# Mamba stage: which states turn by plain products, and where the input projection's last step stands

## The chip, the cores and the metric

The kernel runs on one core of a Trainium2 chip. The metric is the device time of one execution in microseconds (us). A core has a matrix engine (TensorE, PE in the profile, with its weight loads shown as PEld), a vector engine (VectorE, DVE), an activation engine (ScalarE, ACT), a general engine (GpSimd, POOL) and queues for DMA transfers. The engines run side by side, each through its own list of instructions, and wait for one another by semaphores. TensorE writes to PSUM, a small memory of banks that VectorE and ScalarE read; everything else stands in SBUF. The profile also says which share of its full clock TensorE was granted.

## The reference

The program is a vision model of four layers on a tensor of 2 images x 256 channels x 32 x 32: a stage of two Mamba blocks, a local attention by dilated 7x7 convolution, linear attention with a mixture of experts, and softmax attention with a mixture of experts. Only the Mamba stage is touched here. Its core is, for each of the two blocks:

```python
xs, res = split(u @ in_w + in_b)              # 1024 tokens per image, 512 inner channels each
xs = silu(causal_conv4(xs) + conv_b)
dt, Bm, Cm = split(xs @ xproj_w)              # 16, 16 and 16 columns
delta = softplus(dt @ dt_w + dt_b)
dA = exp(delta[..., None] * A)                # 16 states for each channel
dBu = delta[..., None] * Bm[:, :, None, :] * xs[..., None]
hst = dA_t * hst + dBu_t                      # token after token
y_t = einsum('bdn,bn->bd', hst, C_t)
out = ((y + xs * Dp) * silu(res)) @ out_w + out_b
```

The block's output is normed and added to its input; the second block sees the channels in reverse order.

## The kernel before

**Units and slots.** `layer0` (L710) goes over eight units, u0 to u7: two blocks of four chunks of 512 tokens each. For each unit `Mamba.scan` (L488) goes over 16 states and, within a state, four groups of 128 channels: 64 slots, numbered 0 to 63 as 4n + dc. In each slot ScalarE writes the decay exp(delta A) of one state and one group into one of three PSUM banks (m_da, L558), and VectorE runs the recurrence over 512 tokens with one scan instruction (L562), in place over m_h. GpSimd has filled m_h with delta B x before, 1024 columns at a time (L174), into six buffers, which is three states.

**Turning a state.** The scan leaves a state as channels x tokens, but its weighting with C is by token. So `rest(n)` (L507) turns it: four groups (one for each 128 tokens) of four 128x128 pieces, on TensorE, into a ring of three PSUM banks (m_ht). It runs during the slots of the next state: state 7 in slots 32 to 35, 10 in 44 to 47, 11 in 48 to 51, 13 in 56 to 59, and 14 in 60 to 63; state 15 falls into slots 0 to 3 of the next unit. Line 515 chooses between two ways of turning a piece. For a state in `PLAIN` (L264) it is an ordinary matmul with the identity as the moving operand (L516), which in 32-bit floats is two instructions; otherwise it is a transpose (L518), which is one. VectorE then multiplies the group by C's column and adds it to m_ya (L532); for states 0, 3, 6 and 9 ScalarE does this step (L530).

**What runs between.** After each slot's scan the code takes one step of `before` (the turning of the last state) and one of `between`, a list made by `paced` (L687): each entry is a generator with the number of steps to take, the first slot and the end, and the steps are spread evenly between these. The entries are:

- `front` of the next chunk: the convolution with four diagonal taps (m_conv, L373), silu, the projection to dt, B and C (m_xd_ps, L395), the delta matmuls (m_dt, L431), and ScalarE's functions for softplus (L436 and L440 for each of four groups, then L445, L447, L452, L454);
- `enter` of the chunk after that: the input projection, four steps of two matmuls with 512 columns (m_in, L343), each with a copy by ScalarE (m_pre, L347). In u0 to u5 the four steps stand at slots 37 to 45 (`ENTER`, L782);
- `back` of the chunk before: the gate (m_g, L590), the sum (m_y, L619 and L624; read by L628), the output projection (m_out, L635 and L639), its batch-norm statistics on VectorE (L183), and the norm's transposes (mm_t, L204);
- weights of the convolution of the next layer, turned on TensorE (w1t, L871; taps_ps, L877).

The last unit has no next chunk. In its place it carries the early part of the next layer's convolution (early_acc, L933), 112 steps in slots 3 to 63.

**What sets the order.** The code's order above is the wish; a tile scheduler then puts each engine's instructions into a queue, so that an edit can also move neighbours. Each engine then works its queue in order.

Of the kernel before, what the change touches and what calls it, by code (L numbers as in the profile page):

```python
# [258 lines left out]
class Mamba:  # L259
# [1 line left out]


    ADDED = 3, 6, 9
    PLAIN = 10, 13, 14  # L264
    LATER = 3
    ENTER = 4
    HEAD = 12
# [220 lines left out]
    def scan(self, j, before, between, start=False, last=False):  # L488

        net, nc, m, scanp = self.net, self.net.nc, self.m, self.scanp
        xs, bd, ct, delta, du = self.chunks[j]
        state, first = self.state, self.first(j)
        ya = self.two.tile([P, TPC, DI], F32, tag="ya", name=f"{m}_ya_{j}")
        yb = self.one.tile([P, TPC, DI], F32, tag="yb", name=f"{m}_yb_{j}")
        self.chunks[j] = xs, ya, yb
        G = 2  # L500
        half = [P, G, TC]

        def keep(n, hs):
            for g, h in enumerate(hs):
                nc.scalar.copy(state[:, n, g * G : (g + 1) * G], h[:, :, TC - 1])

        def rest(n, hs):  # L507


            for i in range(TPC):  # L510
                ps = self.ps_ht.tile([P, DI], F32, tag="ht", name=f"{m}_ht_{j}_{n}_{i}")
                for dc in range(NDC):
                    a = ps[:, dc * P : (dc + 1) * P]
                    h = hs[dc // G][:, dc % G, i * P : (i + 1) * P]
                    if n in self.PLAIN:
                        nc.tensor.matmul(a, lhsT=h, rhs=net.ident, start=True, stop=True)  # L516
                    else:
                        nc.tensor.transpose(a, h, net.ident)  # L518
                yield
                c = ct[:, i, n : n + 1]  # L520
                to = ya if n == 0 else None
                if n in self.ADDED:
                    if i == 0:
                        aside = self.tail(f"{m}_s_{j}_{n}")[:, : TPC * DI]
                        self.due[n + self.LATER] = (
                            yb, aside.rearrange("p (i d) -> p i d", d=DI), n != self.ADDED[0]
                        )
                    to = self.due[n + self.LATER][1]
                if to is not None:
                    nc.scalar.activation(to[:, i, :], ps, AF.Copy, scale=c)  # L530
                else:
                    nc.vector.scalar_tensor_tensor(  # L532
                        ya[:, i, :], ps, c, ya[:, i, :], ALU.mult, ALU.add
                    )
                if i == 0 and first:
                    keep(n, hs)

        for n in range(NS):
            b = scanp.tile([P, TC], F32, tag="b", name=f"{m}_b_{j}_{n}", bufs=4)
            nc.sync.dma_start(b, bd[n].partition_broadcast(P))  # L540
            hs = []
            for g in range(NDC // G):
                h = scanp.tile(half, F32, tag="h", name=f"{m}_h_{j}_{n}_{g}", bufs=6)
                factors = du[:, g * G : (g + 1) * G, :], b.unsqueeze(1).to_broadcast(half)
                if start and n == 0:
                    nc.vector.tensor_mul(h, *factors)
                else:
                    net.lined(nc.gpsimd.tensor_mul, h, *factors)
                hs.append(h)
            if n in self.due:  # L550
                to, a, add = self.due.pop(n)
                op = ALU.add if add else ALU.bypass
                net.lined(nc.gpsimd.dma_start, to, a, accum_op=op)
            for dc in range(NDC):
                da = self.ps_da.tile([P, TC], F32, tag="da", name=f"{m}_da_{j}_{n}_{dc}")
                i = dc * NS + n
                with net.tc.issue_after(net.loaded.ins):
                    net.decayed = nc.scalar.activation(  # L558
                        da, delta[:, dc, :], AF.Exp, scale=self.aneg[:, i : i + 1]
                    )  # L560
                h = hs[dc // G][:, dc % G, :]
                nc.vector.tensor_tensor_scan(  # L562
                    h, da, h, 0.0 if first else state[:, n, dc : dc + 1], ALU.mult, ALU.add
                )


                next(before, None)
                if n or dc:
                    next(between, None)
            before = chain(before, rest(n, hs))  # L570
        for _ in between:
            pass
        self.due = {} if last else {self.LATER: (ya, yb, True)}
        return before
# [135 lines left out]
def layer0(net, x, x_dram, m1, m2, load_image, taps, conv_dram, lg):  # L710
# [5 lines left out]
    with (  # L716
# [34 lines left out]
        for u, (m, j) in enumerate(units):  # L751
# [4 lines left out]
            steps = [(b, NDC, 4, 20) for b in done]  # L756
# [9 lines left out]
            enters = []  # L766
# [12 lines left out]
            for n, first, end in Mamba.STEPS:  # L779
                steps += [(f, n, first, end) for f in fronts]  # L780
            steps += [(b, 8, 48, 56) for b in done]
            steps += [(e, Mamba.ENTER, 37, 45) for e in enters]  # L782
            steps += [(b, 2, 1, 4) for b in late] + [(b, 2, 9, 15) for b in late]
            steps += [(b, 1, 57, 58) for b in done]
            if u + 1 == len(units):
# [993 lines left out]
def conv_attn_hybrid(ctx: ExitStack, tc: tile.TileContext, a: dict, out: bass.AP):  # L1779
# [6 lines left out]
    with tc.tile_pool(name="conv_w", bufs=2) as convw:  # L1786
        def load_x(b):
            for cc in range(NCC):
                nc.sync.dma_start(x[:, cc, b, :], a["x"][b, cc])

        load_x(0)
        taps = Taps(net, convw, main, x, a["l1_w1"], a["l1_w2"])
        layer0(
            net, x, a["x"],
            [a[f"m1_{k}"] for k in ("in_w", "out_w", "xproj_w", "dt_w")],
            [a[f"m2_{k}"] for k in ("in_w", "out_w", "xproj_w", "dt_w")],
            lambda: load_x(1), taps, conv_dram, lg,
        )
# [117 lines left out]
```

## Time and profile before

| | before |
|---|---|
| median of 3 runs (lowest to highest) | 2128.23 us (2127.43 to 2129.8) |
| the profiled execution's own time | 2127.49 us |
| its span, first to last instruction | 2125.8 us |
| busy: TensorE, VectorE, ScalarE, GpSimd | 1882.2, 1373.1, 900.9, 1042.0 us |
| mean granted TensorE clock | 0.933 |
| Mamba stage: first scan, last scan | 51.4 us, 1018 us |
| lengths of u0 to u7, first scan to next first scan | 108.8, 120.1, 119.9, 122.1, 114.5, 118.2, 114.7, 148.3 us |

In the table, a unit's length runs from its first scan to that of the next unit, and for u7 to the end of its last scan. A line of groups in the profile names the code line, the engine, the operation, its output and inputs, and the shape with its count; then the busy time and the mean length of one; then the engine's idle time just ahead of these instructions and what ended it. A line of waits names the waiting engine and line, whom it waited for, the sum, the number and the longest. A line of a timeline gives the start, the length and the instruction, with the number of like ones in a row; in brackets stands the idle time ahead of it.

### The profile page before, as it was taken

The numbers are of one execution on the slowest core, as the hardware profiler recorded it, in microseconds if no ns is written. First come the engines' busy times: TensorE is split into PE (matmuls) and PEld (weight loads), VectorE is DVE, ScalarE is ACT, GpSimd is POOL, SyncE is SP. The second block draws the span as 40 slices with busy tenths as digits, with TensorE's granted clock in tenths as the row PEclk, the third lists the DMA queues.
The fourth block names the chain that finished last, engine by engine and source line by source line (L and its number), as shares of the span: only waits on it lengthen the run. The fifth ranks groups of instructions, "written<-read, shape, count | busy, mean of one in ns | idle before, by whom it ended". The sixth has DMA issues, their size and how long they took to land.

```text
span 2125.8 us, 27536 instructions
## 1 busy us (share of the span) xinstructions
PE 1882.2 (89%) x9812; PEld 1352.4 (64%) x9812; DVE 1373.1 (65%) x2118; ACT 900.9 (42%) x1626; POOL 1042.0 (49%) x701
## 2 busy tenths in 40 slices
PE   7788988888889988899999899859999699769996
PEld 3365655656565656556655555549998477569994
DVE  6999999999999999984422757642222634532223
ACT  4777777576777677553112533211111222201111
POOL 3797889878898988853324500023332000023331
PEclk9979999998999999999999999969999899879997
DMA  3233324232423323421210100049996200069997
GB/s 112 72 99 88 96 69 113 63 92 69 112 75 98 83 79 93 97 74 25 52 19 1 65 1 10 30 156 326 322 331 261 83 10 10 21 245 330 325 329 288
DMA packets 94964, 256.39 MB, mean 121 GB/s; under 512 B 35964, under 2 KB 52225, under 8 KB 80229
## 3 DMA queue, kind: packets, MB, share of 16 engines
q1 hardware_dynamic: 77636, 198.29, 27.8%
q0 software_dynamic: 12192, 51.66, 9.5%
q10 hardware_dynamic: 4992, 4.59, 0.7%
q8 instruction: 82, 1.34, 0.3%
q14 instruction: 62, 0.50, 0.1%
HBM read 204.60 MB, written 19.37 MB: 105 GB/s over the span
## 4 chain that ended last, share of the span: by engine, by line
PE 47%; DVE 26%; issue 13%; ACT 6%; POOL 4%; DMA 4%; POOLq 0%; DVEq 0%; ACTq 0%
DVE m_h L562 13%; PE h L1723 6%; DVE m_ya L532 6%; PE acc L933 4%; PE o L1737 3%; PE m_ht L518 3%; PE early_acc L933 3%; PE av L1447 3%; PE h L1270 3%; PE sc L1421 2%; DMA l_yd<-y,target 2%; POOL x L1693 2%; PE m_ht L516 2%; POOL l_yd L1743 2%; PE m_out L639 1%
## 5 line engine op out<-in xcount | busy, mean ns | idle before, releaser
L174 POOL TENSOR_TENSOR m_h<-m_du,m_b 128x1024 f32<-128x1024 f32 x254 | 595.8, 2374 | 182.5 <-PE m_ht L518 89.6
L558 ACT ACTIVATE m_da<-m_delta,m_aneg 128x512 f32<-128x512 f32 x512 | 349.7, 692 | 190.9 <-DVE m_h L562 188.2
L1693 POOL DMA_INDIRECT x<-l_zd,source x82 | 84.0, 1025 | 576.6 <-issue 220.7
L518 PEld LDWEIGHTS m_ht<-ident,m_h 128*128 128x128 f32 x1664 | 200.6, 146 | 220.0 <-issue 69.7
L562 DVE TENSOR_TENSOR_SCAN m_h<-m_da,m_state,m_h 128x512 f32<-128x512 f32 x256 | 317.7, 1271 | 21.9 <-ACT m_da L558 15.2
L518 PE MATMUL m_ht<-ident,m_h 128*128 128x128 f32 x1664 | 272.7, 288 | 64.6 <-DVE m_ya L532 31.8
L562 DVE TENSOR_TENSOR_SCAN m_h<-m_da,m_h 128x512 f32<-128x512 f32 x256 | 302.4, 1212 | 7.9 <-ACT m_da L558 7.4
L1723 PEld LDWEIGHTS h<-xts,we 128*128 128x128 f32 x2528 | 298.9, 195 | 5.5 <-issue 1.7
L1723 PE MATMUL h<-xts,we 128*128 128x128 f32 x2528 | 299.4, 278 | 1.5 <-issue 1.5
L532 DVE SCALAR_TENSOR_TENSOR m_ya<-m_ht,m_ct,m_ya 128x512 f32<-128x512 f32 x384 | 276.4, 735 | 32.5 <-PE m_ht L518 16.9
L1730 DVE TENSOR_TENSOR hid<-hid,h 128x512 f32<-128x512 f32 x79 | 54.3, 687 | 267.1 <-PE h L1723 263.5
L1729 ACT ACTIVATE hid<-h 128x512 f32<-128x512 f32 x79 | 47.2, 597 | 414.5 <-PE h L1723 414.5
L516 PE MATMUL m_ht<-ident,m_h 128*128 128x128 f32 x768 | 130.6, 319 | 39.1 <-DVE m_ya L532 25.8
L516 PEld LDWEIGHTS m_ht<-ident,m_h 128*128 128x128 f32 x768 | 115.3, 224 | 62.7 <-DVE m_ya L532 26.3
L1737 PE MATMUL o<-we,hid 128*128 128x256 f32 x632 | 150.7, 381 | 3.9 <-DVE hid L1730 2.3
L1743 POOL DMA_INDIRECT l_yd<-y,target x79 | 79.1, 1001 | 135.3 <-DVE y L1742 131.6
L1737 PEld LDWEIGHTS o<-we,hid 128*128 128x128 f32 x632 | 113.9, 191 | 17.6 <-DVE hid L1730 2.9
L373 PE MATMUL m_conv<-m_pre,m_taps 128*128 128x512 f32 x240 | 115.3, 594 | 0.0
L933 PE MATMUL early_acc<-x,early 128*98 128x448 f32 (+24 forms) x308 | 98.8, 446 | 0.0
L933 PE MATMUL acc<-x,pair 128*98 128x416 f32 (+21 forms) x308 | 94.4, 455 | 0.0
L1742 DVE COPY y<-o 128x256 f32<-128x256 f32 x79 | 33.6, 425 | 69.5 <-PE o L1737 69.3
L639 PE MATMUL m_out<-m_out_sb,m_xs 128*128 128x256 f32 x256 | 73.9, 414 | 0.0
(318 smaller groups left out, 2857.9 us busy)
## 6 DMA issues: line engine op xcount, KB each, us to landing
we<-in_l_experts_dram SPq DMA_DIRECT2D x82, 1536.0 KB, 9.2
m_b<-m_bd SPq DMA_DIRECT2D x128, 256.0 KB, 3.2
m_yb<-m_s POOLq DMA_DIRECT2D x24, 1024.0 KB, 8.6
m_ya<-m_yb POOLq DMA_DIRECT2D x7, 1024.0 KB, 8.5
w<-in_l_w_dram SPq DMA_DIRECT2D x21, 256.0 KB, 3.0
l_zd<-l_z SPq DMA_DIRECT2D x7, 512.0 KB, 2.9
l_yl<-l_yd SPq DMA_DIRECT2D x10, 256.0 KB, 4.7
l_yl<-l_yd ACTq DMA_DIRECT2D x10, 256.0 KB, 5.8
```

Source lines behind the costliest of these rows:

```text
L174: self.line = do(*args, **named)
L373: nc.tensor.matmul(ps, lhsT=self.taps[:, dc * 4 + k, :], rhs=pre[:, dc, k : k + TC], start=(k == 0), stop=(k == 3),)
L516: nc.tensor.matmul(a, lhsT=h, rhs=net.ident, start=True, stop=True)
L518: nc.tensor.transpose(a, h, net.ident)
L532: nc.vector.scalar_tensor_tensor(ya[:, i, :], ps, c, ya[:, i, :], ALU.mult, ALU.add)
L558: net.decayed = nc.scalar.activation(da, delta[:, dc, :], AF.Exp, scale=self.aneg[:, i : i + 1])
L562: nc.vector.tensor_tensor_scan(h, da, h, 0.0 if first else state[:, n, dc : dc + 1], ALU.mult, ALU.add)
L933: nc.tensor.matmul(a[:, lo - 16 * k : hi - 16 * k, co : co + n], lhsT=lhsT, rhs=self.x[:, kc, b, lo - r0 : hi - r0, ci : ci + n], start=(u ...
L1693: nc.gpsimd.indirect_dma_start(out=x, out_offset=None, in_=zd[:, :], in_offset=bass.IndirectOffsetOnAxis(ap=source[:, g : g + 1], axis=0), ...
L1723: nc.tensor.matmul(ps[:, at], lhsT=w12[:, s, kc, at], rhs=xt[:, kc * P : (kc + 1) * P], start=(kc == 0), stop=(kc == NCC - 1),)
L1737: nc.tensor.matmul(ps[:, :C], lhsT=ht[:, mc * P : (mc + 1) * P], rhs=w[:, 8 + mc, :], start=(mc == 0), stop=(mc == NHC - 1),)
L1743: nc.gpsimd.indirect_dma_start(out=yd[g], out_offset=bass.IndirectOffsetOnAxis(ap=target[:, g : g + 1], axis=0), in_=y, in_offset=None, bo ...
```

## The change

Three things are edited.

1. The states turned by products are 7, 11, 13 and 14 instead of 10, 13 and 14: state 7's 16 pieces (slots 32 to 35) and state 11's (48 to 51) become products, and state 10's (44 to 47) become transposes.
2. In the last unit every state is turned by transposes. There are now seven units with four such states, 448 products, where there were eight with three, 384.
3. Of the four steps of `enter` in u0 to u5, three stand at slots 36 to 44, and the last is taken at slot 60.

```diff
-    PLAIN = 10, 13, 14
+    PLAIN = 7, 11, 13, 14
     LATER = 3
     ENTER = 4
...
-                    if n in self.PLAIN:
+                    if n in self.PLAIN and not last:
                         nc.tensor.matmul(a, lhsT=h, rhs=net.ident, start=True, stop=True)
                     else:
                         nc.tensor.transpose(a, h, net.ident)
...
             steps += [(b, 8, 48, 56) for b in done]
-            steps += [(e, Mamba.ENTER, 37, 45) for e in enters]
+            steps += [(e, Mamba.ENTER - 1, 36, 44) for e in enters]
+            steps += [(e, 1, 60, 61) for e in enters]
             steps += [(b, 2, 1, 4) for b in late] + [(b, 2, 9, 15) for b in late]
```

## The prediction

> **What bounds the kernel now.** I read the costliest groups first, then the Mamba stage cut into windows, then VectorE's waits, then the timeline of the slots that the edits touch. The groups (busy us, mean ns of one, idle before):
>
> ```profile
> L518 PE MATMUL m_ht<-ident,m_h 128*128 128x128 f32 x1664 | 272.7, 288 | 64.6 <-DVE m_ya L532 31.8
> L516 PE MATMUL m_ht<-ident,m_h 128*128 128x128 f32 x768 | 130.6, 319 | 39.1 <-DVE m_ya L532 25.8
> L562 DVE TENSOR_TENSOR_SCAN m_h<-m_da,m_state,m_h 128x512 f32<-128x512 f32 x256 | 317.7, 1271 | 21.9 <-ACT m_da L558 15.2
> L532 DVE SCALAR_TENSOR_TENSOR m_ya<-m_ht,m_ct,m_ya 128x512 f32<-128x512 f32 x384 | 276.4, 735 | 32.5 <-PE m_ht L518 16.9
> ```
>
> The 768 instructions of L516 are 384 products: each is two passes. TensorE overlaps, so means of one mislead; I use distances between starts. In the windows (columns: length, then busy PE, PEld, DVE, ACT, POOL with counts, granted clock, DMA share, GB/s):
>
> ```profile
> 160.00:870.00 710.00, 626.58 (x3082) 418.32 (x3081) 676.89 (x761) 511.52 (x868) 610.33 (x308) 0.93 0.34 88
> ...
> 940.00:1020.00 80.00, 78.62 (x334) 46.61 (x333) 50.05 (x62) 28.31 (x42) 33.12 (x17) 1.00 0.15 38
> 1020.00:1055.00 35.00, 33.74 (x223) 27.74 (x221) 10.42 (x30) 3.14 (x8) 7.61 (x12) 1.00 0.08 21
> ```
>
> For the first seven chunks (units u0 to u6, to 870 us) VectorE is the limit: 676.9 of 710 us. In the last, u7, and its tail TensorE is: 112.4 of 115 us from 940 on. So an edit that only takes TensorE time is worth everything in u7 and nothing in u0 to u6, except where VectorE waits. Its waits from 51 to 870 us:
>
> ```profile
> DVE m_h L562 <- ACT m_da L558: 19.7, 20, 4.0
> DVE m_xs L628 <- PE m_y L624: 6.1, 9, 2.2
> DVE ln_st L183 <- PE m_out L639: 5.0, 3, 2.1
> DVE m_ya L532 <- PE m_ht L516: 4.5, 4, 2.5
> ```
>
> The largest is ScalarE late with the decay at slots 40 to 44. The third is a clock matter, seen when the same slots 48 to 51 of u3 and u5 are put side by side, after the slots 44 to 47 of u3:
>
> ```profile
> 481.14:487.82 6.68, 6.68 (x43) 4.76 (x41) 6.68 (x8) 5.57 (x10) 6.60 (x5) 1.00 0.41 87
> 487.82:498.57 10.75, 10.69 (x41) 7.82 (x40) 8.53 (x11) 8.41 (x12) 9.87 (x5) 0.68 0.45 104
> ...
> 720.78:729.11 8.33, 8.10 (x42) 5.66 (x42) 8.33 (x11) 8.33 (x12) 8.33 (x4) 1.00 0.56 118
> 746.33:754.96 8.63, 5.79 (x29) 5.28 (x28) 8.62 (x11) 4.59 (x10) 6.77 (x4) 0.53 0.13 32
> ```
>
> Equal work took 10.75 us at clock 0.68 and 8.33 at 1.00; TensorE is full in both. The last line, u5's slots 60 to 63, is at 0.53.
>
> [...] half-clock stretches are 3.4, 6.8 or 10.2 us long. [...]
>
> **Prices.** From starts in the timeline: at full clock a 128-column transpose comes every 109 ns, a product's pass every 112 (224 a product), a 512-column projection matmul every 430; at half clock a product's pass takes about 213 and the projection matmul about 860. A state of 16 pieces as products instead of transposes: 16 × (224 − 109) = 1.84 us more TensorE time, some 3.6 at half clock.
>
> **A. The last chunk in transposes.** States 10, 13, 14 lose 48 products there: 48 × 115 ns = 5.5 us. The queues show no other move in u7 beyond neighbours. TensorE idles about 1 us at line 518 and 516 in 940 to 1055, so nearly all of it counts[...]. VectorE waits there behind TensorE (20 us at L532), and 6.6 us for GpSimd's m_h, which could become the limit for a short while. I take −5 (−5.5 to −3).
>
> **B. The projection's fourth step at slot 60.** In u0 to u5 four matmuls and one ScalarE copy (m_pre, L347, 0.69 us) move from slot 43 to 60. In the instruction order of the changed kernel the matmuls stand between the halves of state 14's last group (u1 to u5), so that group's last half comes 4 × 0.43 = 1.72 us later, or 3.44 at half clock, which slots 60 to 63 have in all of these units. TensorE is idle about 2 us in these slots, but ahead of the place, in waits for a free m_ht bank, so it covers nothing. What covers is the distance from that group to its reader. In u3 and u4:
>
> ```profile
> 519.69 1.92 PE L516 MATMUL m_ht<-ident,m_h 128*128 128x128 f32 x8
> ...
> 523.46 0.72 DVE L532 SCALAR_TENSOR_TENSOR m_ya<-m_ht,m_ct,m_ya 128x512 f32<-128x512 f32 x1
> ...
> 636.50 1.06 PE L516 MATMUL m_ht<-ident,m_h 128*128 128x128 f32 x4
> ...
> 638.02 0.72 DVE L532 SCALAR_TENSOR_TENSOR m_ya<-m_ht,m_ct,m_ya 128x512 f32<-128x512 f32 x1
> ```
>
> That is 523.46 − 521.61 = 1.85 and 638.02 − 637.56 = 0.46 us; u0 to u5 read 1.1, 1.9, 0, 1.85, 0.46, 1.4. Price less cover: at full clock 0.6, 0, 1.7, 0, 1.3, 0.3 = 3.9 us; at half (u0 full) 0.6, 1.5, 3.4, 1.6, 3.0, 2.0 = 12.1. Behind the waiting L532 stand the next chunk's scans, so VectorE loses it. I take +5.5, nearer the low end[...]. If the scheduler's cover is larger than read, 0. No DMA moves with the step.
>
> **C. Slots 36 to 44.** One of four projection steps leaves (a 0.57 us start-to-start copy on ScalarE, 1.72 us on TensorE) [...]: u3 had 0.63 at 462 to 470 and then waited 5.2 us where others wait 3. Against that, in u2 to u6 ScalarE's queue now has state 10's first decay (in u2, u4 and u6 the second also) ahead of the delta's Abs and Relu. The decay has three banks and must wait for the scan of slot 37 or 38, and the chain L445 to L454, which the VectorE stall at 40 to 44 waits through, starts 1.7 us (odd) or 2.9 us (even) later. By unit, u0 to u6: −0.5, −0.5, 0, −1.2, +1.2, +1, −0.6: −0.6 in all, with ends of −8 and +5.
>
> **D. Slots 44 to 52.** State 10 leaves 1.84 us of TensorE time in 44 to 47, where VectorE doesn't wait (6.68 busy of 6.68): gain 0. Instead some 7.5 us there now hold only transposes, delta matmuls and taps[...]. State 11's 16 products and m_out fall just there: at full clock 8.10 of 8.33 us is already taken, so +1.84 doesn't fit, and at half clock the products are 6.8 us. In odd units the batch-norm statistics move from slot 51 to 57, so u1 and u3 lose their 2.1 us wait, but L532's readers of state 11 and 12 behind products and m_out get about 3.6: +1.5 each. u5, undisturbed before, gets 3.6 at even odds: +1.8. u2, u4 and u6 get 0 to 1.84, I take 0.5 each. Sum +6.3 (−5 if the clock stays and the wait only goes, +12 if every unit pays in full).
>
> **E. State 7 as products, slots 32 to 35.** 1.84 us against 0.3 to 0.9 us of TensorE idle there and 1.4 in the next four slots; L628's wait for m_y grows by 0.3 in even units. +1 (0 to +4).
>
> **Sum:** −5 + 5.5 − 0.6 + 6.3 + 1 = +7.2 on the profiled execution's own 2127.49 us (2125.8 span and 1.7 around it), 2134.7; the runs' median is 0.7 above that execution, so 2135.4. About 0.2% (4.3 us) is what a measurement of this kernel can tell from no change.
>
> **Rivals.**
> *Faster: the clock holds in the middle* (chance 0.31). [...] Then D is −2 × 2.1, C about −2.8 (the leaving copies, 0.57 × 5), B 1 [...], A −5: −11, 2117. For it: u5 at 1.00 with the same delta matmuls[...]. It decides from no half-clock window in slots 44 to 52 of three odd units; with one it turns to my forecast.
> *Same: gains and losses cancel* (0.19). A −5, B at the full-clock price 3.9, C −2, D +3: about 0, 2128. For it: VectorE waits only some 38 us in seven units, so little is to be had; against it: the prices of B and D have one sign.
> *Slower by more: both new places at half clock* (0.14). A −4, B 12, D 10, C 0: +18, 2146. For it: slots 60 to 63 at 0.5 already; against it: covers of 1 to 2 us.
>
> **Numbers.** Forecast 0.36, around 2135 (2131 to 2141). All slower cases 0.50, same 0.19, faster 0.31. The range 2117 to 2146 reaches to both outer rivals and leaves their far halves out.
>
> **What would show it.** A: TensorE busy near 73 of what was 940 to 1020, u7 shorter by 5 us. B: VectorE waits at L532 for L516 in slot 0 or 1 of u1 to u6, 1 to 3 us each. C: the wait for m_da at 40 to 44 about 3 us a unit still. D: clock 0.5 to 0.7 at slots 46 to 50 in most units and L532 waiting on L516 there, no 2.1 us wait of L183. I am wrong if those windows read 1.00, if slot 0 shows no new wait, or if GpSimd takes over in u7.

## The result, and the profile after

The changed kernel takes 2147.79 us (median of four runs, 2144.43 to 2152.27), the kernel before 2129.02 (four runs, 2127.43 to 2129.85). The ratio is 1.0084 with a 95% interval of 1.0065 to 1.0103: slower by 17.9 us (13.8 to 21.9). The forecast was slower by 7.2; the measured median lies 1.8 us above the upper end of the range. The profiled execution of the changed kernel is the longest of its four, 2152.27 us with a span of 2150.6 and a mean clock of 0.920, so its waits add up to somewhat more than the median shows.

From first scan to next first scan, u0 to u6 are longer by +5.0, +0.7, +4.8, −1.0, +6.9, +2.2 and +5.2 us, together 23.8; u7 is shorter by 2.2; what follows the Mamba stage, where no code was changed, is longer by 3.2. The loss is thus spread over the first seven units. The groups of the changed kernel first (busy us, mean ns of one, idle time before them and what ended most of it):

```profile
L518 PE MATMUL m_ht<-ident,m_h 128*128 128x128 f32 x1600 | 252.9, 286 | 53.1 <-DVE m_ya L532 26.5
L516 PE MATMUL m_ht<-ident,m_h 128*128 128x128 f32 x896 | 159.5, 328 | 41.5 <-DVE m_ya L532 24.6
L562 DVE TENSOR_TENSOR_SCAN m_h<-m_da,m_state,m_h 128x512 f32<-128x512 f32 x256 | 316.7, 1270 | 23.5 <-ACT m_da L558 16.2
L532 DVE SCALAR_TENSOR_TENSOR m_ya<-m_ht,m_ct,m_ya 128x512 f32<-128x512 f32 x384 | 279.6, 753 | 48.4 <-PE m_ht L518 29.9
```

The counts are those of the edit: 64 transposes fewer and 64 products (128 passes) more. The scans take as long as before; what has grown is the idle time ahead of VectorE's L532, from 32.5 to 48.4 us. The same three windows as before, moved to where the units now begin (length, busy PE, PEld, DVE, ACT, POOL with counts, clock, DMA share, GB/s):

```profile
165.00:894.00 729.00, 650.16 (x3179) 441.36 (x3178) 671.31 (x761) 516.60 (x869) 607.30 (x306) 0.90 0.34 85
964.00:1044.00 80.00, 78.30 (x312) 43.42 (x311) 52.73 (x67) 28.63 (x42) 34.94 (x19) 1.00 0.16 40
1044.00:1079.00 35.00, 32.32 (x206) 26.16 (x204) 8.47 (x33) 4.09 (x11) 8.58 (x21) 0.95 0.19 37
```

In the first, VectorE's idle time has gone from 33.1 us of 710 to 57.7 of 729, and the clock from 0.93 to 0.90. Between 50 and 900 us TensorE stood at half clock for 177 us, before for 137. VectorE's waits in u0 to u6 (us in total, times, longest) say for whom:

```profile
DVE m_h L562 <- ACT m_da L558: 31.9, 23, 5.2
DVE m_ya L532 <- PE m_ht L516: 17.9, 16, 2.4
DVE m_ya L532 <- PE m_ht L518: 8.1, 13, 2.2
DVE m_xs L628 <- PE m_y L624: 5.4, 7, 1.7
DVE ln_st L183 <- PE m_out L639: 2.0, 2, 1.0
```

Three of these moved. The wait for ScalarE's decay grew from 19.7 to 31.9 us, 15.5 and 27.0 of it at slots 40 to 44; that for turned groups (L516 and L518) from 6.6 to 26.0; the batch-norm wait fell from 5.0 to 2.0. For before, the line that goes with these is

```profile
DVE m_ya L532 <- PE m_ht L518: 2.1, 5, 0.6
```

The moved step can be seen at the end of u2, in TensorE's timeline (start, length, instruction, number in a row):

```profile
409.03 1.19 PE L516 MATMUL m_ht<-ident,m_h 128*128 128x128 f32 x4
410.01 3.40 PE L343 MATMUL m_in<-x,m_in_sb 128*128 128x512 f32 x4
413.25 0.60 PE L872 MATMUL w1t<-ident,w 128*128 128x128 f32 x4
413.68 0.61 PE L516 MATMUL m_ht<-ident,m_h 128*128 128x128 f32 x4
```

and in VectorE's, where the brackets hold the idle time ahead of the instruction:

```profile
414.33 0.75 DVE L532 SCALAR_TENSOR_TENSOR m_ya<-m_ht,m_ct,m_ya 128x512 f32<-128x512 f32 x1 [2.30 <-PE m_ht L516]
```

The four projection matmuls stand between the halves of state 14's last group, at a granted clock of 0.55 (3.40 us; at the end of u5 1.91 us at 0.99), and its reader waits 2.30 us with the next chunk's scans behind it: the scan behind it reads a decay that ScalarE had written by 411.59 us, but starts only at 415.00, after that L532. At the ends of u1 to u5 this wait is 1.54, 2.30, 1.47, 1.98 and about 0.1 us, 7.4 in all; u5 is the one where the four matmuls took 1.91 us instead of 3.1 to 3.4, those at 0.55 to 0.61. At the end of u0 L532 waits 1.17 us too, but not behind the projection: there the scheduler has put the step's matmuls about ten slots earlier (at 137.90 and 139.87 us).

Slots 44 to 47 and then 48 to 51, of u3 (first two lines) and of u5:

```profile
493.10:499.12 6.02, 5.09 (x22) 2.85 (x21) 6.02 (x8) 6.02 (x11) 6.02 (x4) 0.94 0.21 42
499.12:507.86 8.74, 8.74 (x49) 7.65 (x48) 8.74 (x12) 6.95 (x9) 8.66 (x5) 0.85 0.63 135
...
734.86:740.87 6.01, 5.05 (x23) 2.84 (x22) 6.01 (x7) 6.01 (x11) 6.01 (x4) 0.99 0.18 42
740.87:749.74 8.87, 8.87 (x46) 7.66 (x46) 8.74 (x11) 6.96 (x9) 8.79 (x5) 0.81 0.72 160
```

Slots 44 to 47 now leave TensorE about 1 us idle in these two, at a clock of 0.94 and 0.99, and over the four slots after them it is 0.85 and 0.81; in u5 it was 1.00 there. All seven units now have a half-clock stretch about here: the clock over slots 48 to 51 is 0.72 to 0.85. But VectorE is busy through 48 to 51 in u3 (8.74 of 8.74), where before it waited 2.2 us.

In u7, the same 80 us of VectorE's waits as the window from 964 on:

```profile
DVE m_ya L532 <- PE m_ht L518: 16.6, 11, 3.0
DVE m_h L562 <- POOL m_h L174: 6.9, 4, 2.3
DVE m_h L562 <- ACT m_da L558: 2.9, 1, 2.9
```

Before, in the window from 940 on, they were

```profile
DVE m_ya L532 <- PE m_ht L516: 10.8, 7, 3.3
DVE m_ya L532 <- PE m_ht L518: 9.5, 7, 3.0
DVE m_h L562 <- POOL m_h L174: 6.6, 4, 2.3
```

So the groups cost 20.3 us before and 16.6 now, GpSimd 6.6 and 6.9. From u7's first scan to the start of the last matmul of its output projection it was 179.01 us and is now 174.51: 4.5 us less.

### The profile page after: what moved, and what is told of

It is laid out like the page before. It is cut to its first block, busy times and chain, and to the rows that moved or that the text cites. A ratio compares the mean times of both kernels' runs of the same rounds, so it can differ in the third digit from the quotient of the medians.

```text
span 2150.6 us, 27664 instructions
## 1 busy us (share of the span) xinstructions
PE 1911.7 (89%) x9876; PEld 1378.0 (64%) x9876; DVE 1367.6 (64%) x2118; ACT 906.9 (42%) x1626; POOL 1044.0 (49%) x701
## 4 chain that ended last, share of the span: by engine, by line
PE 47%; DVE 25%; issue 13%; ACT 6%; DMA 4%; POOL 4%; POOLq 0%; DVEq 0%; SPq 0%; ACTq 0%
DVE m_h L562 13%; PE h L1724 6%; DVE m_ya L532 6%; PE acc L934 4%; PE o L1738 3%; PE m_ht L516 3%; PE m_ht L518 3%; PE av L1448 3%; PE h L1271 3%; PE sc L1422 2%; PE early_acc L934 2%; DMA l_yd<-y,target 2%; POOL x L1694 2%; PE m_in L343 2%; POOL l_yd L1744 2%
## 5 line engine op out<-in xcount | busy, mean ns | idle before, releaser
L562 DVE TENSOR_TENSOR_SCAN m_h<-m_da,m_h 128x512 f32<-128x512 f32 x256 | 303.7, 1233 | 20.8 <-ACT m_da L558 19.7
L518 PEld LDWEIGHTS m_ht<-ident,m_h 128*128 128x128 f32 x1600 | 193.9, 146 | 185.2 <-issue 68.5
L532 DVE SCALAR_TENSOR_TENSOR m_ya<-m_ht,m_ct,m_ya 128x512 f32<-128x512 f32 x384 | 279.6, 753 | 48.4 <-PE m_ht L518 29.9
L518 PE MATMUL m_ht<-ident,m_h 128*128 128x128 f32 x1600 | 252.9, 286 | 53.1 <-DVE m_ya L532 26.5
L516 PE MATMUL m_ht<-ident,m_h 128*128 128x128 f32 x896 | 159.5, 328 | 41.5 <-DVE m_ya L532 24.6
L516 PEld LDWEIGHTS m_ht<-ident,m_h 128*128 128x128 f32 x896 | 140.1, 231 | 73.6 <-DVE m_ya L532 24.8
L373 PE MATMUL m_conv<-m_pre,m_taps 128*128 128x512 f32 x240 | 114.4, 595 | 0.0
L343 PE MATMUL m_in<-x,m_in_sb 128*128 128x512 f32 x128 | 75.5, 721 | 3.5 <-ACT m_pre L347 2.2
```

The costliest lines, as they stand in the source:

```text
L343: nc.tensor.matmul(ps, lhsT=self.in_sb[:, kc, mc * P : (mc + 1) * P], rhs=self.xt[:, kc, tok], start=(kc == 0), stop=(kc == NCC - 1),)
L532: nc.vector.scalar_tensor_tensor(ya[:, i, :], ps, c, ya[:, i, :], ALU.mult, ALU.add)
L562: nc.vector.tensor_tensor_scan(h, da, h, 0.0 if first else state[:, n, dc : dc + 1], ALU.mult, ALU.add)
```

## The experiments

The theory after the result: the moved projection step (B) costs most; states 11 for 10 (D) some; the last chunk (A) gives about 4 back. The rival: D costs most by the clock, B little. All ratios are to the kernel before, with 95% intervals; 0.001 is 2.1 us. Where an expectation quotes an earlier run (+13.6 for the projection edit, say), it is the difference of two medians, which can lie some 2 us from what the ratio gives.

**Each edit alone.** The projection edit, as in the change, with the states of before:

```diff
-            steps += [(e, Mamba.ENTER, 37, 45) for e in enters]
+            steps += [(e, Mamba.ENTER - 1, 36, 44) for e in enters]
+            steps += [(e, 1, 60, 61) for e in enters]
```

> Only the input projection's fourth step is moved to slot 60. Theory 1 (this step is the largest part): the matmuls in front of state 14's last group make L532 wait 1.5 to 2.3 us in slot 0 of u2 to u5, 7 to 9 us in all, and the next chunk's convolution, one group later, costs some 5 us more around slots 20 to 24: +8 to +14 us. Theory 2 (state 7's products are the largest part): +4 to +8, and the waits for m_da at slots 40 to 44 stay at the 3 us a unit of the kernel before.

Measured: 1.0056 (1.0038 to 1.0074), +11.9 us. Two thirds of the loss come from this edit alone. The waits at the units' ends came to 7.0 us in all, as expected, but the rest does not lie at slots 20 to 24: it is found at slots 40 to 44, as shown further below.

The last chunk alone:

```diff
-                    if n in self.PLAIN:
+                    if n in self.PLAIN and not last:
```

> Only the last chunk is turned by transposes throughout. My prediction said -5 us, since TensorE was full there. The profile of the changed kernel shows u7's scans only 2.2 us shorter. Theory 1 (what TensorE gives back is used by the convolution's matmuls that stood behind, and the end of the stage still comes early): -4 to -5.5. Theory 2 (GpSimd's m_h, for which VectorE waits at slots 44, 48, 52 and 56, takes part of it): -1.5 to -3.

Measured: 0.9987 (0.9978 to 0.9996), −2.8 us. Up to the start of the last matmul of the output projection u7 takes 174.49 us, as in the changed kernel, 4.5 less than before. The interval of the whole (−4.7 to −0.9) holds this 4.5, so whether some of it is lost again later isn't shown.

The states alone, first 7 added, then 11 in place of 10 without 7:

```diff
-    PLAIN = 10, 13, 14
+    PLAIN = 7, 10, 13, 14
```

> State 7 is turned by products in addition to 10, 13 and 14, in all eight units; nothing else. Theory 1 (state 7's products come ahead of the delta matmuls on TensorE; ScalarE's queue then holds state 10's first decays ahead of the Abs and Relu of the second pair, and the chain L445 to L454 comes later): m_da waits at slots 40 to 44 of 5 to 6 us instead of 3 in the even units, +6 to +12. Theory 2 (they only cost TensorE time [...]): -3 to +3.

Measured: 1.0005 (0.9991 to 1.0019), +1.1 us: no difference shown, although the waits for the decay at slots 40 to 44 grew here too, from 15.5 to 21.9 us in u0 to u6.

```diff
-    PLAIN = 10, 13, 14
+    PLAIN = 11, 13, 14
```

> State 11 is turned by products instead of state 10, in all eight units; nothing else. My prediction's part D: half clock at slots 46 to 50 in most units and +6 us. Theory 2, from the changed kernel's profile (slots 44 to 56 of the units together cost only about 1 us more there, because the transposes save in 44 to 47 what the products cost in 48 to 51): -2 to +2, although the clock does fall.

Measured: 1.0016 (1.0006 to 1.0026), +3.4 us. D costs, about half of what was forecast, and less than the projection edit: the rival is out. The four together give 11.9 − 2.8 + 1.1 + 3.4 = 13.6 us; the whole change has 17.9 (13.8 to 21.9).

**Is it the place of the fourth step, or the three others moved from 37 to 36?** The three steps stay where they were (slots 37, 39, 41), and the fourth goes to S:

```diff
-            steps += [(e, Mamba.ENTER, 37, 45) for e in enters]
+            steps += [(e, Mamba.ENTER - 1, 37, 43) for e in enters]
+            steps += [(e, 1, S, S + 1) for e in enters]
```

S = 60:

> The kernel before with the fourth projection step at slot 60 and the other three kept where they were (slots 37, 39 and 41). Theory 1 (only the place at slot 60 costs): L532 waits 1 to 3 us in slot 0 or 1 of the units, 5 to 8 us in all, the waits for m_da at slots 40 to 44 fall to the before level of about 3 us a unit, and the time is +5 to +9 us where the whole edit was +13.6. Theory 2 (any removal of the fourth step from slot 43 reorders the engines' queues around slots 36 to 44, and that is half of the loss): +11 to +15, with m_da waits of 4 to 6 us in even units as in the run with the whole edit.

S = 56:

> As the kernel with the three steps kept, but the fourth at slot 56, where TensorE idles about 3 us in the slots 56 to 59. Theory 1 (the cost at 60 is that the matmuls stand between state 14's last pieces and their reader at half clock): the waits of L532 in slot 0 go, and it is 4 to 8 us faster than with the step at slot 60. Theory 2 (wherever it stands late in the unit, some group of a product state waits): the wait moves to state 13's readers, and the time is within 3 us of that at slot 60.

S = 62:

> The kernel before with three projection steps kept at slots 37, 39 and 41 and the fourth at slot 62, where in TensorE's queue it comes behind all of state 14's pieces instead of between them. Theory 1 (the wait in slot 0 comes from the matmuls between the pieces): L532's waits for L516 fall from 10.6 us with the step at slot 60 to the 4 to 5 us of the kernel before, and the time is 3 to 6 us below that run's +9: +3 to +6. Theory 2 (the same delay falls on state 15's pieces and on the next chunk's convolution): L532 waits for L518 instead, and the time stays at +8 to +12.

S = 44:

> The kernel before with the fourth projection step one slot later, at 44 instead of 43. Theory 1 (what makes the waits for m_da at slots 40 to 44 longer, 18.9 to some 26 us, is that the convolution and y of the same unit come later because of the step at the unit's end): m_da waits stay at 17 to 21 us and the time within 2 us. Theory 2 (that the step left slot 43 is what does it): m_da waits of 23 us and more, +4 to +8.

| fourth step at | ratio | interval | us |
|---|---|---|---|
| 44 | 0.9999 | 0.9989 to 1.0009 | −0.2 |
| 56 | 1.0066 | 1.0047 to 1.0085 | +14.1 |
| 60 | 1.0033 | 1.0022 to 1.0045 | +7.0 |
| 62 | 1.0071 | 1.0056 to 1.0086 | +15.1 |

The place of the one step decides: at 44 nothing, from 56 on 7 to 15 us. Slot 56 does not escape, although it lies four slots ahead of the group that was read as its only victim. At 62 the wait moves to the next groups, those of state 15: L532 waits 2.2, 1.4 and 0.5 us for L518 in slot 1 of u2, u3 and u5. The expectation that leaving slot 60 would help was wrong both times. And at 60 the waits for the decay at slots 40 to 44 did not fall back to the old level, but came to 21.9 us. Whether the three other steps, one slot earlier in the change, add to the loss isn't told: 7.0 us (4.7 to 9.6) without that and 11.9 (8.1 to 15.8) with it overlap.

**The change without its projection edit, and what remains if it is mended.** First the changed kernel with the old line for the projection:

> The changed kernel with the projection's four steps back in slots 37 to 45: states 7, 11, 13, 14 by products and the last chunk in transposes. If the edits add up, the last chunk's -2.9, state 7's +1.5 and state 11's +3.5 give +2 us. If they interact [...], +6 to +10.

Measured: 1.0000 (0.9992 to 1.0009). States and last chunk cancel to within 2 us; the whole loss hangs on the projection edit.

States 7, 10, 13, 14 in u0 to u6 and transposes in u7:

> States 7, 10, 13 and 14 by products in u0 to u6 and the last chunk in transposes; the projection as before. Theory 1 (the last chunk's gain stands alone; state 7 in u0 to u6 is worth about nothing): -1 to -4 us. Theory 2 (state 7's products [...] gain in u2 and u3, as the profile with state 7 added shows, 5.8 us there): -5 to -8.

Measured: 0.9981 (0.9965 to 0.9997), −4.0 us: with the last chunk alone the fastest seen, though the two aren't told apart. With the fourth step at 44 besides:

> The parts that did no harm, together: the last chunk in transposes, states 7, 10, 13 and 14 by products in u0 to u6, the fourth projection step at slot 44. If the parts add (-3.5 and -1.2): -3 to -7 against before.

Measured: 1.0007 (0.9992 to 1.0022); the gain that was expected did not come. The two intervals overlap a little, so that the step at 44 takes the gain away isn't shown either. And the whole change with the three steps kept and the fourth at 62:

> The changed kernel with the three projection steps at slots 37, 39 and 41 and the fourth at 62. If the place of the projection is the whole loss and 62 is harmless, the time is that of the changed kernel without the edit: 0 to +4 against before. If leaving slots 36 to 45 costs wherever it goes: +10 to +15.

Measured: 1.0086 (1.0072 to 1.0100), as the change itself.

**Do the projection edit and state 11 make each other worse?** Both, without state 7 and with the last chunk as before:

> The projection edit and state 11 in place of 10, without state 7 and with the last chunk as before. Alone they cost +13.6 and +3.5. If they only add: +17. If state 11's products at half clock behind the shifted queues are what makes the whole (+18.8) larger than its parts (13.6 + 3.5 + 1.5 - 2.9 = 15.7): +19 to +22, with L532's waits for L516 at 15 us and more.

Measured: 1.0060 (1.0047 to 1.0074), +12.8 us, where the two alone add up to 15.3. That they make each other worse isn't seen; this theory fell.

**Is it the crowd on the two shared banks?** The projection, convolution, delta, y, output and weight-turning matmuls share two PSUM banks (m_mm). If more users at the end of a unit were the cause, one more step of the next layer's weights there would cost as much:

```diff
-                for n, first, end in ((2, 12, 32), (4, 35, 47), (3, 58, 63)):
+                for n, first, end in ((2, 12, 32), (3, 35, 47), (4, 58, 63)):
```

> The kernel before with the projection untouched, but one step of the next layer's weight turning (w1t or taps_ps, a short user of the m_mm banks) moved from slots 35 to 47 to slots 58 to 63. Theory 1 (one more user of the two m_mm banks at the unit's end makes the convolution late): +4 to +10, convolution 1 us and more later in u2 to u6. Theory 2 (it is the length of the projection's matmuls and their place): -2 to +2.

Measured: 1.0003 (0.9991 to 1.0015). And taking two of these steps away should make room for the projection at 60:

```diff
+            steps += [(e, Mamba.ENTER - 1, 37, 43) for e in enters]
+            steps += [(e, 1, 60, 61) for e in enters]
...
-                for n, first, end in ((2, 12, 32), (4, 35, 47), (3, 58, 63)):
+                for n, first, end in ((4, 12, 32), (4, 35, 47), (1, 58, 63)):
```

> The fourth projection step at slot 60 as in the run at60 (+9), and two of the three weight-turning steps moved from slots 58 to 63 to slots 12 to 32. Theory 1 (the number of users of the m_mm banks at the unit's end): the convolution starts as before, and the time falls to 0 to +4 above its control, the kernel with these two steps moved alone. Theory 2 (the projection's matmuls themselves): it stays 6 to 12 us above the control.

with the last line's edit alone as its control:

> Control: the kernel before with two weight-turning steps moved from slots 58 to 63 to slots 12 to 32, the projection untouched. Both theories: within 4 us of the kernel before; less work at the unit's end, more where TensorE has some idle time.

Measured: 1.0065 (1.0046 to 1.0083) against 1.0005 (0.9993 to 1.0018) for the control. More room did not help, and one user more did no harm: the number of users of these banks doesn't explain the loss. The convolution did start nearly as in the kernel before (later by 0.1, 1.0, 0, 0.8 and 1.6 us in u2 to u6), and the loss stayed.

**Is it the step's presence at the end, or its absence at 43?** The four steps as before, and the fourth's matmuls and copy once more at slot 60:

```diff
-        for mc in range(NDC):
+        for mc in (*range(NDC), *[NDC - 1] * again):
...
+            steps += [(e, 1, 60, 61) for e in enters]
```

> The kernel before with its four projection steps where they were, and the fourth computed a second time at slot 60 (same values, so TensorE and ScalarE do one step more in six units). Theory 1 (its absence from slot 43 costs): 0 to +5 us. Theory 2 (its presence at the unit's end costs): +9 to +15, with L532's waits in slot 0 and 1.

Measured: 1.0052 (1.0040 to 1.0064), +11.1 us. The step's presence at the end costs, with slot 43 filled as before. (A second computation at a neutral slot was not run, so the price of the added work alone is not known.) The opposite, the fourth step gone from u0 to u5 and its quarter filled by a copy on GpSimd:

```diff
-        for mc in range(NDC):
+        for mc in range(NDC - short):
...
+                net.lined(nc.gpsimd.tensor_copy, pre[:, mc + 1, 3:], pre[:, mc, 3:])
```

> Left out: the fourth step of the input projection in u0 to u5 (a quarter of that projection); GpSimd copies the third quarter in its place at slot 41, so that TensorE and ScalarE have no fourth step at all. Theory 1 (its absence from slot 43 costs, by the order of the queues): +4 to +10, although there is less work. Theory 2 (its presence at the end costs): -4 to +2.

Measured: 1.0241 (1.0228 to 1.0254). This run says nothing on the question: the copy stands in GpSimd's queue ahead of m_h (VectorE waited 25.3 us for it), and the layers after the stage, which got other data, are 23.6 us longer.

**Where the rest of the loss sits.** Where the step does no harm (at 44), VectorE's waits in u0 to u6 are these:

```profile
DVE m_h L562 <- ACT m_da L558: 19.7, 20, 3.4
...
DVE m_ya L532 <- PE m_ht L518: 4.0, 7, 1.1
...
DVE m_ya L532 <- PE m_ht L516: 1.2, 2, 0.9
```

With the projection edit alone:

```profile
DVE m_h L562 <- ACT m_da L558: 25.7, 22, 5.3
DVE m_ya L532 <- PE m_ht L516: 11.1, 13, 2.8
DVE m_ya L532 <- PE m_ht L518: 6.4, 8, 1.6
```

With the step done twice:

```profile
DVE m_h L562 <- ACT m_da L558: 30.5, 25, 5.4
DVE m_ya L532 <- PE m_ht L516: 7.3, 7, 2.3
DVE m_ya L532 <- PE m_ht L518: 6.7, 9, 1.6
```

So VectorE's waits grew in two places. One is the end of the unit, where L532 waits for the interrupted group: 6.1 us at the ends of u1 to u5 in the projection edit alone, and 0.9 at that of u0, of the 10.9 by which its waits for groups grew. The other is the decay at slots 40 to 44 of the unit after it. Summed over u0 to u6, VectorE waits there 15.5 us in the kernel before and 15.1 with the step at 44, but 22.4 with the edit alone, 25.8 with the step done twice and 27.0 in the whole change. Of the whole change without its projection edit it is 20.0, so the edit adds 7 us there with the old states and with the new. How that decay comes to be late can be followed in ScalarE's waits of the projection edit alone:

```profile
ACT m_pre L347 <- PE m_in L343: 10.9, 10, 2.1
...
ACT m_e L436 <- DVE m_xs L628: 6.8, 5, 4.6
```

Neither the kernel before nor the one with the step at 44 has the second line; the one with the step done twice has the same 6.8 us. The last quarter of m_pre, which used to be ready 35 to 40 us before the unit ends, is now written 0.9 to 3.6 us after the next has begun (u2 to u6). In u2 to u6 the next convolution (L373) then starts 2.6, 4.4, 3.0, 5.2 and 2.7 us after the unit's first scan, before at 1.1, 3.0, 1.0, 1.7 and −0.2; and ScalarE stands idle ahead of the delta's first function (L436) until VectorE's L628, for 4.6 us in u2 and for 0.55 in each of four others. In u4 of this kernel ScalarE reads

```profile
588.43 0.69 ACT L436 ACTIVATE m_e<-m_dt,cols_sb 128x512 f32<-128x512 f32 x1 [0.55 <-DVE m_xs L628]
...
596.02 0.69 ACT L347 ACTIVATE m_pre<-m_in,cols_sb 128x512 f32<-128x512 f32 x1 [1.37 <-PE m_in L343]
596.60 1.14 ACT L452 ACTIVATE m_du<-m_e,one 128x1024 f32<-128x1024 f32 x1
```

while TensorE had

```profile
592.36 3.62 PE L343 MATMUL m_in<-x,m_in_sb 128*128 128x512 f32 x4
```

and VectorE at slot 41

```profile
600.80 1.22 DVE L562 TENSOR_TENSOR_SCAN m_h<-m_da,m_h 128x512 f32<-128x512 f32 x1 [5.30 <-ACT m_da L558]
```

The projection of the chunk after, a step left in slots 36 to 44, runs at half clock here (0.50 from 592 to 596 us; 3.62 us against 1.88 in the kernel before); its copy holds up L452, whose input L447 had written by 594.65 us and which starts at 596.60, behind that copy, and with it the delta that the next decay is made from; the wait is 5.30 us, before 2.13.

This chain is read from the traces; that it makes the loss is not shown. Three runs speak against it as a general account. With state 7 added and the projection untouched, VectorE's wait for the decay in u0 to u6 was

```profile
DVE m_h L562 <- ACT m_da L558: 25.2, 19, 3.5
```

21.9 us of it at slots 40 to 44, nearly as long as with the projection edit, and no difference in time was shown: other waits had become shorter (for L516 from 4.5 to 2.2 us, the batch-norm wait from 5.0 to 2.1). With the extra weight step at the unit's end the convolution of u2 and u4 was late by 2.5 and 2.3 us, but at slots 40 to 44 VectorE waited 17.0 us, and the time was not measurably longer. And with the step at 60 and two weight steps taken away (+13.8 us) it waited there only 16.6 us; what grew, by 11.7 us, were its waits for turned groups:

```profile
DVE m_ya L532 <- PE m_ht L516: 12.2, 9, 3.8
...
DVE m_ya L532 <- PE m_ht L518: 6.2, 11, 1.0
```

So the runs show that the step costs when it stands at the unit's end, and that nothing is lost at 44. Which of VectorE's waits take the time varies from kernel to kernel. In the changed kernel itself ScalarE stood at L436 for L628 only 2.1 us, so the late decay there must have more causes than the one followed here. Why slot 60 with the three steps kept costs half of what 56 and 62 cost stays open; the traces can't settle it, because the profiled execution is the slowest of the runs at 60 (2142.95 us, median 2138.07) and the fastest of those at 56 (2137.84, median 2145.72).

## Why the prediction was right or wrong

| step | forecast, us | measured alone, us |
|---|---|---|
| A, last chunk in transposes | −5 | −2.8 (−4.7 to −0.9) |
| B and C, projection | +5.5 − 0.6 | +11.9 (8.1 to 15.8) |
| D, 11 for 10 | +6.3 | +3.4 (1.3 to 5.5) |
| E, state 7 | +1 | +1.1 (−1.9 to +4.0) |
| all | +7.2 | +17.9 (13.8 to 21.9) |

**The sign was right, the size too small, and B with C is the step that failed:** +4.9 us forecast, +11.9 measured. It failed in two places, the second by more.

The first is "I take +5.5, nearer the low end", that is, nearer the full-clock price; that choice was an estimate. In u1 to u4 of the changed kernel the four matmuls took 3.1 to 3.4 us at a granted clock of 0.55 to 0.61, and only in u5 1.91 us at 0.99. The forecast's own price less cover, taken at the clock that each of these units had, is 1.5 + 3.4 + 1.6 + 3.0 + 0.3 = 9.8 us; the waits there were 7.4. The distances to the reader were thus right to within about 1 us a unit, and the clock was taken too high. In the projection edit alone the four matmuls took 1.96 to 3.62 us and the waits came to 6.1. So this part was short by 2 us at most.

The second is that the cover was sought for one reader, "the distance from that group to its reader". The step has a second consumer, the next chunk's convolution, and its result, once 35 to 40 us early, now comes 0.9 to 3.6 us into the unit that needs it. C looked at slots 40 to 44 for the step that leaves them and for state 10's decays in ScalarE's queue, put the late result at nothing, and gave −0.6. In the traces the waits for the decay there grew by 6.9 us (22.4 − 15.5) in the projection edit alone, and by 11.5 in the whole change, 4.5 of it without the projection edit. That B lacked a cost of the step's late place is shown by the runs at 44, at 56 and with the step done twice; that it runs through the convolution is the reading of the traces above, and stays open.

The prediction's reading of the clock had gaps too. One half-clock stretch, from slot 48 of u0 on (133.18 to 153.66 us), is 20.5 us long. In u3 half clock (0.50) follows on two quite different stretches: at slot 48 on 3.41 us (from 484.75) in which TensorE was busy for 3.35, mostly with delta matmuls and transposes, and at slots 60 to 63, on which B rests, on 3.41 us (from 512.06) in which it was busy for only 1.65, with products alone. Where B, C and D expected one clock or the other, that was the author's estimate: the traces show where half clock stood, not what brings it.

**A was right in its mechanism and in its stage** (−4.5 us against −5; TensorE's waits in u7 fell, and GpSimd's grew by 0.3 us only). Of the whole execution −2.8 is measured, with an interval that holds −4.5.

**D was right in sign and in the clock, too large in size.** All seven units have the half-clock stretch (granted clock 0.58 to 0.81 over slots 46 to 50 in the changed kernel), with D alone too (0.71 to 0.89 over slots 48 to 51). With D alone VectorE's idle time in these slots went from 6.2 to 9.0 us in all. In u1, u3 and u5 it was 0.9, 2.2 and 2.1 us, before 2.1, 2.2 and 0; the net is −1.2, 0 and +2.1 against the forecast's +1.5, +1.5 and +1.8. The batch-norm waits of u1 and u3 went, as said, but the late groups took 0.9 to 2.2 us and not 3.6. u2 and u4 paid 1.2 and 0.9 against 0.5. The gain of 0 in slots 44 to 47 was read from u3: in u2 VectorE had waited 3.0 us there behind state 10's products, and with D alone it no longer does. **E** is within what the run can tell.

**The rivals.** "The clock holds in the middle" needed full clock in three odd units and is out: u1, u3 and u5 read 0.78, 0.85 and 0.81 over slots 48 to 51. "Gains and losses cancel" came true for everything but the projection, 1.0000. "Slower by more" at 2146 is nearest in the sum and right about the half clock at the step (0.55 to 0.61 in u1 to u4), but that its sum fits is luck: its B of 12 stood for the waits at the units' ends, which were 6 to 9 us, and its D of 10 measured 3.4. Against the list of what would show each step: the waits for L516 at the unit's end came, in u1 to u4 between 1.5 and 2.3 us; the wait for the decay at slots 40 to 44, 2.2 us a unit before (15.5 over seven), rose to 3.9 (27.0).

## What to carry to other kernels

When a step is moved later in an in-order queue, list every consumer of its result and by how much each was early, not just the instruction that it is put in front of; here a result that had been 35 to 40 us early came up to 3.6 us into the unit that needs it. Price it at the clock of the place it goes to, as the profile of before shows it there (here 0.50 to 0.60 over slots 60 to 63 of u1 to u5). Don't take the growth of one wait for the loss either: with state 7 added VectorE's waits for the decay grew by 6 us and the time did not. And try a neutral place as well: the same step at slot 44 cost nothing that could be measured, and dropping this one edit of the change gave all of its loss back.

## What the runs showed that was not expected

- Four matmuls of 512 columns, 1.7 us at full clock from the 430 ns between starts, cost 7 to 15 us over six units, that is 1.2 to 2.5 us each on average, at the end of a unit and nothing measurable 16 slots earlier, with VectorE, not TensorE, busy most (676.9 against 626.6 us of 710 in the kernel before).
- The four matmuls, put one after the other, mostly ran below full clock: 3.1 to 3.4 us in four of five units of the changed kernel, at a mean granted clock of 0.55 to 0.61, and 1.91 us at 0.99 in the fifth; in the projection edit alone the same five read 1.96 to 3.62. The half-clock stretches of both traces in the Mamba stage are 3.41, 6.83, 10.24 and, once, 20.48 us long in the kernel before, and 3.41, 6.83, 10.24, 13.65 and 23.89 in the changed one, all multiples of 3.41; what sets their beginning and end is not shown.
- More half clock is not more time by itself: u5's slots 48 to 51 went from 8.33 us at 1.00 to 8.87 at 0.81, with state 11's products in hand besides, and the four slots ahead of them from 6.68 to 6.01, so that the eight together took no longer. With D alone, though, the same slots 48 to 51 took 10.42 us at 0.74.
